# Cross-attention on one core: another order of all operations, and a PSUM bank of its own for the fourth energy product

## The chip, the core and the metric

The kernel runs on one core of one Trainium2 chip. The core has a matrix engine (TensorE; PE in the profile, with its weight loads as PEld), three engines for elementwise work (VectorE, DVE; ScalarE, ACT; GpSimd, POOL), a queue that issues transfers (SyncE, SP), an on-chip memory SBUF and an accumulator memory PSUM of eight banks, each 128 partitions by 512 float32 values. Matmuls write PSUM; ACT and DVE read and write it; POOL works on SBUF alone.

The metric is the device time of one execution in microseconds. The kernel before takes 1973.53 us (median of 3 runs, 1973.33 to 1973.71).

## The reference

For each of 32 samples, with `x` and `y` (the context) of 256 channels by 1024 positions:

```python
x_q = einsum('oc,bcn->bno', w_qk, y)
x_k = einsum('oc,bcn->bon', w_qk, x)
x_v = einsum('oc,bcn->bon', w_v, x) + b_v[None, :, None]
energy = einsum('bnc,bcm->bnm', x_q, x_k)
attention = softmax(energy, axis=-1)
attention = attention / (1e-07 + attention.sum(axis=1, keepdims=True))
x_r = einsum('bcn,bnm->bcm', x_v, attention)
x_r = relu(einsum('oc,bcn->bon', w_t, x - x_r) + b_t[None, :, None])
return x + x_r
```

## The kernel before

**Numbers.** Each float32 operand of a matmul is split into a rounded part (HIGH) and the remainder (LOW). `product` makes one block product of three matmuls, high by high, high by low and low by high, into one bank. So each name with a P below, and each A, is three matmuls of 128x128 weights by 512 columns.

**Blocks of seven products.** The keys (`k`, from `w_qk` twice and x), the energies (`E0` to `E3`) and the part of the output that comes from x (`x`) are made as 2 by 2 blocks with seven products P1 to P7 in place of eight. `chain` says in which bank each accumulates: P1, then P6, then P7 and last P4 in bank `a`, P2 in `b`, P5 and then P3 in `c`. Between them ACT copies the running sum of bank `a` to SBUF three times: `r1` after P1, `r2` after P6, `r3` after P7. DVE then adds these copies to the other banks: `c11` = b + r1, `c22` = c + r3 (before P3 comes on top of c), `c12` = c + r2 (after P3). The fourth block, 21, is what stands in bank `a` after P4.

**One sample's work.** An energy `E<p>` gives a pair of tiles of 128 rows by 1024 columns: tile 2p lies in banks 0 and 1, tile 2p+1 in banks 2 and 3. For these the smallest value of each row is needed, and DVE takes it in the instruction that makes a block: `c22`, `c11`, `c12` add and take the minimum at once; for block 21, which needs no addition, `m21` (`energy_least`) reads bank `a` with a row of zeros as second operand. Then, for tile n with halves h of 512 columns (one bank each): `exp<n>` on ACT over both banks, with the row sums; `ri<n>` on DVE, their reciprocals; for each half `h<n><h>` on ACT (HIGH of the attention weights), `l<n><h>` on DVE (LOW; it needs the result of `h`) and `sum<n><h>` on DVE (adds the tile to the column sums `acc`). `A<n><c><h>` multiplies the values `uf` with these weights into banks 4 to 7. The next pair's P1 can start when the bank that it writes has been read by `h`, `l` and `sum`.

**The rest.** `V<q><half>` makes the values (12 matmuls of 256 columns each), `vh` (ACT) and `vl` (DVE) split them. `cols`, `inv` and `turn` (DVE) turn the column sums into reciprocals, `div<c>` (DVE) divides, `join<c>` (POOL) adds the x part, `pos<c>` (ACT) is the relu, `add<c>` is a transfer on POOL's queue that adds x, `st<c>` (SP) stores. The next sample's operands are prepared meanwhile: `xh`, `yh`, `xTh`, `ysh`, `khD`, `kTh` on ACT, `xl`, `yl`, `xTl`, `ysl`, `klD`, `kTl0`, `kTl1` and the sums `xT`, `ys`, `kT2` on POOL.

**What sets the order.** Three lists of names, `FIRST`, `STEADY` (repeated for samples 1 to 29) and `LAST`. A `+` before a name means the next sample, a `-` the one before. `InOrder` keeps each engine to the order of the list; between engines each instruction waits for what it depends on, and any two accesses of ACT, DVE and PE to one PSUM bank keep the list's order too, two reads included.

Of the kernel before, what the change touches and what calls it, by code (L numbers as in the profile page):

```python
# [17 lines left out]
def kernel(  # L18
# [739 lines left out]
    for c in range(KC):  # L758
# [13 lines left out]
        ys01 Sgram Swt ys03 ys02 Scorner Swtc ys04 Sgh0 Stp Sgh1 Sbvw Fxh0 Sgl xh1 Sgraw  # L772
        Fyh Ssq Fxl0 yh00 Svh Gh12 FHH0 yh01 Fyl yl00 FHL0 FHH1 FLH0 Svl Fxl1 FLH1 yl01
        FHL1 ysh0 Fraw11 Fkh12 V01 V00 V11 Fkh11 ysl0 V10 kT1 Sth Fraw22 vh0 kT2 Th12
        Fkh22 Fkl12 Fkl11 ldy1 kT3 Fkl22 kh21 kT4 kl21 FE11 FE00 yh11 yh10 kTh0 vh1 FE10
        FE01 vl0 vl1 Fmin1 Stl Gl12 kTh1 Sbias Tl12 ys11 exp1 kTl0 Fmin0 +ldx0 ri1 Gs1
        +xT1 h10 sum11 Gs2 kTl1 l10 sum10 FX11 FX01 FX00 E1P1 exp0 ri0 h11 h01 FX10 h00
        E1r1 Fxw0 E1P6 Gh22 l11 l01 sum00 Ts1 ys13 l00 ys12 E1P2 sum01 E1r2 Fxw1 E1P7 E1r3
        E1P5 E1P4 A110 Gs3 E1c11 Ts2 ys14 ysh1 Gl22 E1c22 E1m21 +xh0 exp3 Ts4 E1P3 Ts3
        yl11 Gs4 E1c12 yl10 A101 A010 A111 A100 ri3 h30 exp2 ysl1 h31 sum30 l30 E2P1 A000  # L780
        E2r1 sum31 ri2 E2P6 +ldx1 A011 h21 Th22 l31 sum20 l21 sum21 E2r2 E2P7 h20 GhS E2P5
        l20 E2r3 E2P4 E2c22 E2m21 +xh1 E2P2 ThS E2P3 +xl0 E2c11 +xT3 E2c12 +xTh0 exp5 ri5
        +ldy0 h50 A300 A001 exp4 h51 A301 A200 sum50 l50 E3P1 ri4 E3r1 sum40 +xT2 sum51
        GlS h41 sum41 l51 A500 E3P6 E3r2 A310 h40 +yh00 E3P7 l41 E3r3 +xl1 +ys03 +xT4
        +ys01 E3P5 +yh01 +xTh1 l40 +ldy1 E3c22 E3P4 E3P2 E3m21 TlS +xTl0 E3c11 +ys02 exp7
        E3P3 A311 +ys13 +xTl1 Tl22 E3c12 ri7 h70 sum70 A400 A201 A210 A211 h71 exp6 l70
        l71 +kP1 A510 ri6 sum71 +yl00 +ys04 +kr1 +ysh0 +ys11 +ys12 sum61 +kP6 A511 A501
        h61 +kr2 +yl01 +ys14 l61 +kP7 h60 +yh11 +kP5 sum60 +kr3 l60 +kc22 +ysl0 +kP2 +kc11
        +kP3 +kc12 A401 A410 +kP4 +khD +yl11 +kT1 +yh10 +kh21 A701 A411 +kT2 +klD A700
# [3 lines left out]
        E0P1 -cols ysh1 kTh1 -inv --st0 kTl1 -A610 -A601 -A711 E0r1 kTh0 -turn E0P6 -div0
        E0r2 E0P2 --st1 +ldx0 -A611 kTl0 E0P7 -div1 E0r3 E0P5 E0c22 E0P4 yl10 E0m21 E0c11
        V11 exp1 ri1 E0P3 h10 -join0 ysl1 V10 V00 h11 E0c12 exp0 sum10 l10 sum11 ri0 vh1
        sum01 E1P1 E1r1 h00 V01 h01 vl1 E1P6 E1r2 xP1 E1P7 vh0 +ldx1 l00 l01 sum00 l11
        E1r3 xr1 +xh0 E1P5 E1P2 E1P4 vl0 E1c22 A111 E1m21 exp3 xP2 xP6 E1c11 E1P3 -join1
# [6 lines left out]
        E3c22 A210 E3P4 A510 -add0 +ys11 +xTl1 E3m21 +ysh0 +yh11 E3P3 exp7 E3c12 ri7 A511
        A200 A301 A410 sum70 h70 exp6 l70 sum71 ri6 +kP1 +kr1 A201 sum61 sum60 h61 +yh01
        +kP6 +kr2 h71 h60 A710 l61 +kP5 +kP7 +yh10 +kr3 l60 +kc22 A501 +yl11 +yl00 +ys12
        +ysl0 +ys13 +yl01 +ys14 +kP2 +kP3 l71 A500 +kc11 +khD +kc12 A401 +kP4 A400 A411
        A700 +kT1 +kh21 +kT3 +kT2 +klD +kl21 +kT4 A701 A600
    """
# [80 lines left out]
```

## Time and profile before

| | |
|---|---|
| median of 3 runs | 1973.53 us |
| the profiled execution | 1973.25 us |
| its span, first to last instruction | 1971.5 us |
| PE busy | 1893.3 us (96%) |
| DVE busy | 1606.0 us (81%) |
| ACT busy | 1430.9 us (73%) |
| POOL busy | 1395.1 us (71%) |
| mean granted TensorE clock | 0.999 |

The profile counts an instruction from its start to its end. Matmuls overlap: the next one starts before the one before has ended, and so the distance between starts is what a matmul costs. All instructions of the three compute engines and of PE bear line 62, since `InOrder` issues them; they are told apart by operation and tile: `banks<-gf,yd` is a P1, P2 or P4 of an energy, `banks<-gf,ysum` one of its P3, P5, P6, P7, `banks<-efs,uf` an A, `banks<-xf,gws` a key product, `banks<-xf,tws` an x product, `banks<-vws,xf` a V. On DVE `efs` is an `l`, `acc` a `sum`, and `CUSTOM_DVE_ANT_0` a `c` or `m21` of an energy. On ACT `efs` is an `h`, `banks<-banks,small` an `exp`, `rs<-banks` an `r`.

### The profile page before, as it was taken

The numbers are of one execution on the slowest core, as the hardware profiler recorded it, in microseconds if no ns is written. First come the engines' busy times: TensorE is split into PE (matmuls) and PEld (weight loads), VectorE is DVE, ScalarE is ACT, GpSimd is POOL, SyncE is SP. The second block draws the span as 40 slices with busy tenths as digits, with TensorE's granted clock in tenths as the row PEclk, the third lists the DMA queues.
The fourth block names the chain that finished last, engine by engine and source line by source line (L and its number), as shares of the span: only waits on it lengthen the run. The fifth ranks groups of instructions, "written<-read, shape, count | busy, mean of one in ns | idle before, by whom it ended". The sixth has DMA issues, their size and how long they took to land. (4 is left out here: it accounts for less than half of the span.)

```text
span 1971.5 us, 25233 instructions
## 1 busy us (share of the span) xinstructions
PE 1893.3 (96%) x8680; PEld 1495.7 (76%) x8680; DVE 1606.0 (81%) x3044; ACT 1430.9 (73%) x2223; POOL 1395.1 (71%) x975
## 2 busy tenths in 40 slices
PE   9999999999999999999999999999999999999998
PEld 7777777777777777777777777777777777777776
DVE  6878888788887788887888878888788887888877
ACT  7777777777777777767777777777777777777665
POOL 8876777767677676777677776777767777676672
PEclk9999999999999999999999999999999999999999
DMA  2122212222122231222221232212222122221222
GB/s 94 36 82 75 75 44 75 75 75 75 47 71 75 75 82 47 65 76 83 78 52 56 75 86 75 66 53 76 75 75 75 44 75 75 75 75 50 59 75 75
DMA packets 46722, 136.78 MB, mean 69 GB/s; under 512 B 4480, under 2 KB 5376, under 8 KB 46592
## 3 DMA queue, kind: packets, MB, share of 16 engines
q1 hardware_dynamic: 37248, 102.25, 15.0%
q0 software_dynamic: 8928, 32.51, 9.8%
q8 instruction: 68, 1.11, 0.2%
q14 instruction: 62, 0.51, 0.1%
q10 hardware_dynamic: 416, 0.39, 0.1%
HBM read 101.58 MB, written 33.55 MB: 69 GB/s over the span
## 5 line engine op out<-in xcount | busy, mean ns | idle before, releaser
L62 PE MATMUL banks<-efs,uf 128*128 128x512 f32 x3072 | 780.5, 390 | 0.0
L62 PEld LDWEIGHTS banks<-efs,uf 128*128 128x128 f32 x3072 | 576.7, 188 | 124.2
L62 DVE SCALAR_TENSOR_TENSOR efs<-banks,small,efs 128x512 fp32r<-128x512 f32 x512 | 376.1, 746 | 131.6 <-ACT efs L62 131.5
L62 PE MATMUL banks<-gf,ysum 128*128 128x512 f32 x1524 | 421.1, 398 | 26.8 <-ACT rs L62 25.8
L62 ACT ACTIVATE efs<-banks,small 128x512 fp32r<-128x512 f32 x512 | 340.3, 693 | 122.5 <-DVE acc L62 68.2
L62 ACT COPY rs<-banks 128x512 f32<-128x512 f32 (+1 forms) x475 | 278.0, 585 | 188.2 <-PE banks L62 175.6
L62 PEld LDWEIGHTS banks<-gf,ysum 128*128 128x128 f32 x1524 | 274.1, 188 | 113.3 <-ACT rs L62 55.1
L62 ACT ACTIVATE banks<-banks,small 128x1024 f32<-128x1024 f32 x256 | 278.1, 1086 | 110.0 <-DVE small L62 109.8
L62 PE MATMUL banks<-gf,yd 128*128 128x512 f32 x1158 | 333.8, 400 | 23.3 <-DVE efs L62 20.0
L62 DVE SCALAR_TENSOR_TENSOR acc<-banks,small,acc 128x512 f32<-128x512 f32 x448 | 328.5, 745 | 15.2 <-ACT efs L62 6.9
L62 POOL TENSOR_TENSOR xf<-raws,xf 128x1024 fp32r<-128x1024 f32 x62 | 149.7, 2415 | 208.8 <-ACT xf L62 208.8
L62 PEld LDWEIGHTS banks<-gf,yd 128*128 128x128 f32 x1158 | 206.0, 188 | 99.2 <-DVE efs L62 32.4
L62 POOL TENSOR_TENSOR sums<-raws 128x256 f32<-128x256 f32 (+1 forms) x188 | 187.0, 1003 | 80.5 <-DMA raws<-in_ctx_dram 76.4
L62 POOL TENSOR_TENSOR gf<-sums,gf 128x1024 fp32r<-128x1024 f32 x95 | 227.3, 2408 | 2.1
L62 PE MATMUL banks<-xf,gws 128*128 128x512 f32 x651 | 195.3, 417 | 19.8 <-DVE efs L62 19.7
L62 PEld LDWEIGHTS banks<-vws,xf 128*128 128x128 f32 x1536 | 196.3, 190 | 8.2
L62 PE MATMUL banks<-vws,xf 128*128 128x256 f32 x1536 | 198.5, 282 | 0.0
L62 DVE CUSTOM_DVE_ANT_0 banks<-banks,rs 128x512 f32<-128x512 f32 x254 | 179.0, 705 | 22.2 <-PE banks L62 16.9
L62 PEld LDWEIGHTS banks<-xf,gws 128*128 128x128 f32 x651 | 110.4, 188 | 92.8 <-DVE efs L62 51.8
L62 PE MATMUL banks<-xf,tws 128*128 128x512 f32 x651 | 168.3, 389 | 0.0
L62 POOL TENSOR_TENSOR ysum<-sums,ysum 128x1024 fp32r<-128x1024 f32 x64 | 158.7, 2480 | 8.2 <-ACT ysum L62 8.2
L62 ACT CAST gf<-sums 128x1024 fp32r<-128x1024 f32 x95 | 99.9, 1053 | 76.1 <-DVE sums L62 76.0
(105 smaller groups left out, 2338.6 us busy)
## 6 DMA issues: line engine op xcount, KB each, us to landing
raws<-in_x_dram SPq DMA_DIRECT2D x66, 512.0 KB, 3.2
raws<-in_ctx_dram SPq DMA_DIRECT2D x63, 512.0 KB, 3.8
z<-in_x_dram POOLq DMA_DIRECT2D x62, 512.0 KB, 5.4
out_dram<-z SPq DMA_DIRECT2D x62, 512.0 KB, 4.0
out_dram<-z SPq DMA_DIRECT2D x4, 256.0 KB, 2.0
xe<-in_ctx_dram SPq DMA_DIRECT2D x1, 512.0 KB, 6.7
z<-in_L_xattn_w_t_dram ACTq DMA_DIRECT2D x1, 256.0 KB, 4.4
z<-in_L_xattn_w_v_dram SPq DMA_DIRECT2D x1, 256.0 KB, 5.1
```

The lines of the kernel that those rows point to most:

```text
L62: self.last = getattr(self.engine, name)(*args, **kwargs)
```

## The change

All energies get other banks: `a` is bank 3 and `d` bank 2 (before: `a` bank 2, `d` bank 3). P4 no longer accumulates on bank `a`: it starts a sum of its own in `d`. `c22` now writes to bank `a` instead of `d`. `m21` with its row of zeros goes, and `c21` comes in its place: it adds `r3` to bank `d` and takes the minimum in the same instruction. The tiles lie where they lay.

```diff
-    zeros_row = nc.const_aps.tensor(0.0, [P, MB], F32)
...
-        where = {1: "a", 2: "b", 5: "c", 6: "a", 7: "a", 4: "a", 3: "c"}
+        where = {1: "a", 2: "b", 5: "c", 6: "a", 7: "a", 4: "d" if "d" in bank else "a", 3: "c"}
         for i, w in where.items():
             words[f"{name}P{i}"] = lambda b, i=i, w=w: product(
-                banks[:, bank[w]], left(i), right(i), i in (1, 2, 5)
+                banks[:, bank[w]], left(i), right(i), i in (1, 2, 5) or w == "d"
             )
...
-    EB = dict(a=2, b=0, c=1, d=3)
+    EB = dict(a=3, b=0, c=1, d=2)
...
-    def energy_least(b, p):
-        dve.tensor_tensor_reduce(
-            out=eb["a"],
-            in0=eb["a"],
-            in1=zeros_row,
...
-        return banks[:, EB["a"] : EB["a"] + 2] if n % 2 else banks[:, EB["b"] : EB["b"] + 2]
+        at = EB["bd"[n % 2]]
+        return banks[:, at : at + 2]
...
-        word(f"E{p}c22", energy_block, p, 3, "c", "d", "mB", None)
+        word(f"E{p}c22", energy_block, p, 3, "c", "a", "mB", None)
         word(f"E{p}c12", energy_block, p, 2, "c", "c", "m0", "mA")
-        word(f"E{p}m21", energy_least, p)
+        word(f"E{p}c21", energy_block, p, 3, "d", "d", "m1", "mB")
...
     STEADY = """
...
-        E2P3 -pos1 A110 E2c12 exp5 A311 ri5 A010 A001 sum50 h50 exp4 A300 l50 +yh00 E3P1
...
+        E2P4 xc12 l20 E2r3 E2c22 xw21 +xh1 E2c21 A101 E2P2 A110 E2P3 exp5 E2c11 ri5 E2c12
+        h51 exp4 +ldy0 h50 l51 A001 sum51 A010 ri4 +xTl1 A311 A310 +ys01 h41 E3P1 A300
```

The number of instructions of each kind on each engine is the same before and after. The three lists are new from end to end; in the steady list `sum` stands ahead of `h` for 9 of the 16 halves before, and for 4 of 16 in the change. Three places show how the work moves.

First, PE from the third pair's energy to the fourth's. Before, the `ysum` row just ahead of the long `efs` row is P3, the `yd` row ahead of it P4, and the `yd` row behind the long one the fourth pair's P1:

```order
L62 MATMUL banks<-gf,ysum 128x512 x6
L62 MATMUL banks<-efs,uf 128x512 x3
L62 MATMUL banks<-gf,yd 128x512 x3
L62 MATMUL banks<-gf,ysum 128x512 x3
L62 MATMUL banks<-efs,uf 128x512 x15
L62 MATMUL banks<-gf,yd 128x512 x3
L62 MATMUL banks<-efs,uf 128x512 x6
L62 MATMUL banks<-gf,ysum 128x512 x3
```

In the change the first `yd` row here is P4, the second P2, and the third the next pair's P1:

```order
L62 MATMUL banks<-gf,ysum 128x512 x6
L62 MATMUL banks<-gf,yd 128x512 x3
L62 MATMUL banks<-efs,uf 128x512 x3
L62 MATMUL banks<-gf,yd 128x512 x3
L62 MATMUL banks<-efs,uf 128x512 x3
L62 MATMUL banks<-gf,ysum 128x512 x3
L62 MATMUL banks<-efs,uf 128x512 x12
L62 MATMUL banks<-gf,yd 128x512 x3
L62 MATMUL banks<-efs,uf 128x512 x3
L62 MATMUL banks<-gf,ysum 128x512 x9
```

P4 has moved ahead of P2 and P3, and 27 matmuls in place of 21 lie from the start of P4 to the next P1. Behind P1 one A in place of two lies ahead of P6 (`ysum`).

Second, DVE at the same place, from the reciprocal of tile 5 (the first `RECIPROCAL`) on. Before:

```order
L62 RECIPROCAL small<-small 128x1
L62 SCALAR_TENSOR_TENSOR acc<-banks,small,acc 128x512
L62 SCALAR_TENSOR_TENSOR efs<-banks,small,efs 128x512
L62 RECIPROCAL small<-small 128x1
L62 SCALAR_TENSOR_TENSOR acc<-banks,small,acc 128x512
L62 SCALAR_TENSOR_TENSOR efs<-banks,small,efs 128x512
```

In the change:

```order
L62 RECIPROCAL small<-small 128x1
L62 ISA banks,small<-banks,rs,small 128x512
L62 ISA small 128x1
L62 SCALAR_TENSOR_TENSOR efs<-banks,small,efs 128x512
L62 SCALAR_TENSOR_TENSOR acc<-banks,small,acc 128x512
L62 RECIPROCAL small<-small 128x1
L62 SCALAR_TENSOR_TENSOR efs<-banks,small,efs 128x512
```

`c12` (the `ISA` pair: the addition, and the reading of its minimum) now stands behind the reciprocal, and `l` ahead of `sum`.

Third, POOL, from the `add` transfers to the first energy of the next sample. Before:

```order
L62 DMA z<-in_x_dram 128x1024 x2
L62 TENSOR_TENSOR sums<-raws 128x256
L62 TENSOR_TENSOR xf<-sums,xf 128x1024
L62 TENSOR_TENSOR yd<-raws,yd 128x2x2x128
L62 TENSOR_TENSOR yd<-raws,yd 128x256
L62 TENSOR_TENSOR sums<-sums,raws 128x256
L62 TENSOR_TENSOR ysum<-sums,ysum 128x1024
L62 TENSOR_TENSOR sums<-raws 128x256
L62 TENSOR_TENSOR yd<-raws,yd 128x2x2x128
L62 TENSOR_TENSOR sums<-raws,sums 128x256
L62 TENSOR_TENSOR sums<-sums 128x512
L62 TENSOR_TENSOR gf<-sums,gf 128x1024 x3
```

In the change (behind the last row come the same three `gf` rows, `klD`, `kTl1` and `kTl0`):

```order
L62 DMA z<-in_x_dram 128x1024
L62 TENSOR_TENSOR xf<-sums,xf 128x1024
L62 TENSOR_TENSOR sums<-sums,raws 128x256
L62 TENSOR_TENSOR sums<-raws,sums 128x256
L62 TENSOR_TENSOR sums<-sums,raws 128x256
L62 TENSOR_TENSOR yd<-raws,yd 128x2x2x128
L62 TENSOR_TENSOR sums<-raws 128x256
L62 TENSOR_TENSOR sums<-raws,sums 128x256
L62 DMA z<-in_x_dram 128x1024
L62 TENSOR_TENSOR yd<-raws,yd 128x256
L62 TENSOR_TENSOR ysum<-sums,ysum 128x1024
L62 TENSOR_TENSOR sums<-sums 128x512
```

The two `add` transfers no longer stand together: one has moved down past the `xf` and six more instructions. The last three rows ahead of the `gf` rows are now `yl00`, `ysl0` and `kT2`.

More of the change, by code (lines that the diff above doesn't have):

```diff
@@ L771 @@
     FIRST = """
[L772 to L789, printed above, removed]
@@ L791 @@
+        +yh10 A610 +klD +kTl1 +kh21
     """
     STEADY = """
[L793 to L797, printed above, removed]
@@ L804 @@
[L804 to L808, printed above, removed]
+        E0P1 E0r1 yh11 ysh1 -A700 -A701 -A611 E0P6 -div1 kTl0 -A601 kl21 -A600 E0r2 E0P7
@@ L809 @@
+        sum60 +kr2 +kP7 +kr3 A710 +ysh0 +kP2 +kc22 h71 +kc11 +kP3 +kc12 -st1 A610 +kP4
+        -add0 +yl00 +kT1 +ysl0 +kT2 +kT3 l71 +khD ++ldx0 -st0 +kT4 +kTh0 +klD +kTh1 cols
+        A511 A400 +kh21 inv turn +kTl1 A501 A411 A401 A711
     """
     LAST = """
[L811 to L813 removed]
@@ new lines @@
+        xl1 -A311 -A101 -l20 -sum20 -E2r3 -E2c22 -E2P2 -E2c21 xTh0 xTh1 -exp5 -E2c11 -ri5
+        -A110 -E2P3 xl0 -A001 -A000 -A010 -A301 -h51 -h50 ldy1 -E2c12 ldy0 xTl0 -l51
+        -sum51 -exp4 -E3P1 -ri4 -h41 -E3r1 -A300 -E3P6 -l50 -sum41 -h40 -l41 -E3r2 yh01
+        -sum50 -l40 -sum40 -E3P5 --pos0 -E3P7 -A200 -E3r3 -E3c22 -E3P2 xTl1 ys01 ys11 ys02
+        --add0 --pos1 -E3P4 -A310 -A201 -E3P3 -E3c21 -A501 -A211 yh11 -exp7 -E3c11 -A500
+        -A210 -ri7 -E3c12 -h70 -l70 -sum70 kP1 yh10 -exp6 -ri6 -sum71 ys12 ys14 ys13 yl10
```

99 lines of the change are left out of this document (54 added, 45 removed).

## The prediction, written before the result was known

> **What bounds the kernel now.** I read the page first (engines' shares), then PE in order of time over one sample, then the groups, and then DVE and ACT in order of time at PE's two longest stops.
>
> ```profile
> PE 1893.3 (96%) x8680; PEld 1495.7 (76%) x8680; DVE 1606.0 (81%) x3044; ACT 1430.9 (73%) x2223; POOL 1395.1 (71%) x975
> ```
>
> PE looks full, but its ends overlap. PE in order of time (start, length, how many) over one sample, which runs from its first energy product at 623.55 to the next sample's at 684.46, 60.91 us:
>
> ```profile
> 620.15 3.56 PE L62 MATMUL banks<-efs,uf 128*128 128x512 f32 x15
> 623.55 0.91 PE L62 MATMUL banks<-gf,yd 128*128 128x512 f32 x3
> ...
> 628.40 1.60 PE L62 MATMUL banks<-gf,ysum 128*128 128x512 f32 x6
> 630.03 0.96 PE L62 MATMUL banks<-gf,yd 128*128 128x512 f32 x3
> ...
> 632.96 3.03 PE L62 MATMUL banks<-vws,xf 128*128 128x256 f32 x24
> 635.83 0.86 PE L62 MATMUL banks<-gf,yd 128*128 128x512 f32 x3
> ...
> 653.93 0.84 PE L62 MATMUL banks<-gf,yd 128*128 128x512 f32 x3
> 654.61 0.84 PE L62 MATMUL banks<-gf,ysum 128*128 128x512 f32 x3
> 655.29 3.56 PE L62 MATMUL banks<-efs,uf 128*128 128x512 f32 x15
> 659.50 0.98 PE L62 MATMUL banks<-gf,yd 128*128 128x512 f32 x3 [0.64 <-DVE efs L62]
> 660.32 1.55 PE L62 MATMUL banks<-efs,uf 128*128 128x512 f32 x6
> ...
> 662.39 0.86 PE L62 MATMUL banks<-gf,yd 128*128 128x512 f32 x3
> 664.09 1.65 PE L62 MATMUL banks<-gf,ysum 128*128 128x512 f32 x6 [0.83 <-ACT rs L62]
> ...
> 666.26 0.84 PE L62 MATMUL banks<-gf,yd 128*128 128x512 f32 x3
> ...
> 668.30 2.88 PE L62 MATMUL banks<-efs,uf 128*128 128x512 f32 x12
> 671.81 0.97 PE L62 MATMUL banks<-xf,gws 128*128 128x512 f32 x3 [0.62 <-DVE efs L62]
> ...
> 673.45 0.96 PE L62 MATMUL banks<-xf,gws 128*128 128x512 f32 x3
> ...
> 679.01 0.85 PE L62 MATMUL banks<-efs,uf 128*128 128x512 f32 x3
> ...
> 684.46 0.93 PE L62 MATMUL banks<-gf,yd 128*128 128x512 f32 x3
> ```
>
> Fifteen matmuls take 3.40 us from the first start to the next group's: 0.227 us each, so a product of three costs 0.68. Twenty-four V matmuls take 2.87: 0.12 each. A sample has, by the code, 222 of the first kind (four energies, keys and x part of 21 each, 96 for the output) and 48 of the second: 50.4 + 5.7 = 56.1 us. So PE loses 60.9 - 56.1 = **4.8 us a sample**; nothing in the change alters the 56.1. Where it loses them, from the same rows (distance between starts less 0.227 a matmul):
>
> - A, ahead of the fourth pair's P1 (energy `E3`) at 659.50: 655.29 + 15 x 0.227 = 658.69, so 0.81, and 0.14 more because a product that had to wait takes 0.82 to the next start: 0.95.
> - B, the fourth pair's P7 at 664.09: 1.70 - 0.68 = 1.02, and 0.13 of the same start-up: 1.15.
> - C, the keys' P1 at 671.81: 3.51 - 2.72 = 0.79.
> - D, the keys' other products: 671.81 to 679.01 with 27 matmuls, 7.20 - 6.12 = 1.08.
> - E, the first pair's P4 at 630.03: 1.63 - 1.36 = 0.27, and the start-up: 0.39.
>
> A to E make 4.36; about 0.45 lies in shorter stops (the second pair's P7, mostly). All are waits of PE for ACT and DVE, whose own busy time leaves room (81% and 73%). What they wait for at A, DVE and then ACT in order of time:
>
> ```profile
> 654.82 0.76 DVE L62 CUSTOM_DVE_ANT_0 banks<-banks,const-float32-0.0,small 128x512 f32<-128x512 f32 x1 [0.51 <-PE banks L62]
> 656.91 0.16 DVE L62 RECIPROCAL small<-small 128x1 f32<-128x1 f32 x1 [0.59 <-ACT banks L62]
> 657.11 0.75 DVE L62 SCALAR_TENSOR_TENSOR acc<-banks,small,acc 128x512 f32<-128x512 f32 x1
> 658.69 0.75 DVE L62 SCALAR_TENSOR_TENSOR efs<-banks,small,efs 128x512 fp32r<-128x512 f32 x1 [0.84 <-ACT efs L62]
> ```
> ```profile
> 655.67 1.09 ACT L62 ACTIVATE banks<-banks,small 128x1024 f32<-128x1024 f32 x1 [0.40 <-DVE small L62]
> 657.97 0.69 ACT L62 ACTIVATE efs<-banks,small 128x512 fp32r<-128x512 f32 x1 [1.10 <-PE banks L62]
> 672.81 0.59 ACT L62 COPY rs<-banks 128x512 f32<-128x512 f32 x1 [0.75 <-PE banks L62]
> ```
>
> The third pair's P4 starts at 653.93, `m21` 0.89 later, `exp5` 0.85 after that, `ri5` 1.24, then `sum50`, `h50` (the profile names PE as what it waited for, but `sum50`, on the same bank, ended at 657.86, 0.11 before), `l50`, and P1 0.81 after `l50`'s start: 5.57 us from P4 to the next P1. PE has 21 matmuls, 4.76 us, to cover them. The difference, 0.81, is A. C is the same: from the fourth pair's P4 at 666.26, 21 matmuls cover 4.76 and the keys start 5.55 later. So a loss here is a chain's length less the work that PE finds in the list meanwhile.
>
> **The change part by part.** *Counts and prices.* No instruction goes or comes; `c21` takes the form of `c12`, and `m21` cost as much:
>
> ```profile
> L62 DVE CUSTOM_DVE_ANT_0 banks<-banks,const-float32-0.0,small 128x512 f32<-128x512 f32 x127 | 96.4, 759 | 39.8 <-PE banks L62 30.3
> L62 DVE CUSTOM_DVE_ANT_0 banks<-banks,rs,small 128x512 f32<-128x512 f32 x127 | 96.3, 759 | 26.7 <-PE banks L62 25.9
> L62 ACT ACTIVATE efs<-banks,small 128x512 fp32r<-128x512 f32 x512 | 340.3, 693 | 122.5 <-DVE acc L62 68.2 <-PE banks L62 37.0 <-DVE small L62 15.4
> ```
>
> 759 ns each: nothing. All gain or loss is PE's waiting.
>
> *E, P4 in its own bank.* It no longer waits for `r3`. Its new bank was last read by `kl21` on DVE, which stands between `div1` and `div0` and should end some 1 us ahead of P4. E goes: 0.39 saved (bounds 0 and 0.39).
>
> *A and C, the cover.* In the change the fourth pair's P1 comes 27 matmuls, 6.12 us, after P4's start. The chain: `c21` 0.89 after P4, `exp5` 0.85, `ri5` 1.24, `h51` 0.20, and `l51` 0.72 later, at 3.90. But `c12` stands ahead of `l51` on DVE and needs P3, which starts 2.72 after P4 and is ready at 3.65; `c12` puts `l51` to about 4.35. `sum51` follows 0.67 behind, and P1 0.81 after its start: 5.83. It fits with 0.3 to spare, so A becomes 0 (bounds 0 and 0.4). The keys' P1 again lies 27 matmuls behind its P4; there `c21` waits for `c22`, which waits for `r3` (behind `yh00` and `xTh0` on ACT), and starts about 1.2 after P4; the rest is the same, some 5.8 to 6.0 against 6.12. C becomes 0 (0 to 0.4). This, and not a shorter chain, is where I see the gain: `l` and `sum` still read one bank one after the other.
>
> [...]
>
> *B and D, the steps of bank `a`.* From one product in bank `a` to the next one there a copy on ACT must fit. The keys' P1 at 671.81 is read at 672.81, the copy takes 0.59, and P6 follows at 673.45: 1.64, and about 1.52 where P1 has no start-up of its own. With one other product between, PE has 1.36. So each step with a single product between costs 0.16 to 0.28 and a start-up of 0.13, say 0.35. The new order has six such places a sample: the third pair's P7 (an x product between), the fourth pair's P6 (one A) and P7 (P5), the keys' P6 and P7, and the keys' P3, which needs `c22` after `r3` (about 2.3 us against 2.04). 6 x 0.35 = 2.1. For the second pair's P7 (`r2` behind `vh0` on ACT) I add 0.2, and 0.25 for what stays everywhere: 2.55, where B, D and the short stops have 1.15 + 1.08 + 0.45 = 2.7 now. Bounds of this part: 1.5 (the steps at 0.2) and 3.4 (two late copies more).
>
> *POOL ahead of the next sample.* P1 of the next sample needs `klD`, the first of the three `gf` rows. In the change all of this stands in one line on POOL, from the `add` transfer that waits for `pos1`, which ACT runs right behind the fourth pair's `r3`:
>
> ```profile
> L62 POOL TENSOR_TENSOR gf<-sums,gf 128x1024 fp32r<-128x1024 f32 x95 | 227.3, 2408 | 2.1
> L62 POOL TENSOR_TENSOR ysum<-sums,ysum 128x1024 fp32r<-128x1024 f32 x64 | 158.7, 2480 | 8.2 <-ACT ysum L62 8.2
> L62 POOL TENSOR_TENSOR xf<-sums,xf 128x1024 fp32r<-128x1024 f32 x62 | 153.6, 2477 | 1.5 <-ACT xf L62 1.5
> L62 POOL TENSOR_TENSOR yd<-raws,yd 128x512 fp32r<-128x512 f32 (+1 forms) x126 | 133.3, 1107 | 1.6 <-ACT yd L62 1.6
> L62 POOL DMA_DIRECT2D z<-in_x_dram x62 | 53.8, 878 | 108.0 <-ACT z L62 108.0
> L62 POOL TENSOR_TENSOR sums<-sums,raws 128x256 f32<-128x256 f32 x63 | 50.7, 805 | 2.4
> L62 POOL TENSOR_TENSOR sums<-sums 128x512 f32<-128x512 f32 x32 | 41.4, 1294 | 121.9 <-DVE sums L62 121.9
> ```
>
> Two `add` 1.76, `xf` 2.48, five small `sums` of about 0.85, two `yd` 2.21, `ysum` 2.48, `kT2` 1.29, `klD` 2.41: 16.9 us. Counted from the third pair's P4, the fourth pair's `r3` ends near 11.2 and `pos1` near 12.3, so `klD` ends near 29.1. PE's work from that P4 to the next sample is 27.2, and with 1.7 of stops 28.9: I take 0.2 (bounds 0 and 1.0). Before, POOL stood idle 121.9 us in 31 samples ahead of `kT2`, so there it had 4 us to give.
>
> *Sum.* A 0, C 0, E 0, the steps 2.55, POOL 0.2: 2.75 us a sample against 4.85. That is 2.1 saved, 31 times (the first and the last sample together count as one, having parts of the same stops): 65 us. 1973.25 - 65 = 1908 for an execution like the profiled one, whose time is 0.3 us under the median: **1908 us**. All terms at their lower bounds: 1.5 a sample, 3.35 saved, 1869. At their upper ones: 3.4 + 0.8 + 1.0 = 5.2, 0.35 more than now, 1984.
>
> **The rivals.**
>
> *Only the bank acts, the covers come to nothing.* The spare 0.3 at A and C is small, and one transfer or one late ACT instruction eats it; if A and C move to the next product, E's 0.39 stays: 31 x 0.39 = 12 us, **1961 us**. For it: ACT is strictly in order, and three waits stand ahead of `r2`. Against: 27 matmuls in place of 21 are 1.36 us more cover at both places.
>
> *PE hardly waits.* If ACT's back-to-back starts (672.81 and the like: less than the length of one) keep up better than I reckon, only some 0.3 to 0.8 us a sample stay, 4.2 saved: **1843 us**. Against: with one product between two steps the 1.56 us are a floor.
>
> [...]
>
> *The stops only move.* Same sum in other places, **1973 us**. For it: DVE and ACT have the same work. Against: the two longest stops are worked out as covered.
>
> *Slower: POOL's line becomes the bound.* From the point at which `klD` comes 2.3 us later than I reckon (2.1 saved and 0.2 already counted), each further us costs 31. The second y transfer, asked for only when `xl1` has run, or a later `pos1`, would do it; 1 us beyond is **2004 us**. For it: the line has no slack, where before it had 4 us. Against: POOL's groups have steady durations and its line is counted whole.
>
> **How the numbers follow.** Forecast 0.63, only the bank 0.12, hardly any wait 0.08, moved stops 0.06, slower 0.11. A difference under 0.2% (4 us) can't be told from none. Faster by more: 0.63 + 0.12 + 0.08 = 0.83; within: 0.06; slower: 0.11. The likeliest case's own range is 1885 to 1940; to hold 8 in 10 with the 1961 partly in and half of the fast case: 1875 to 1958.
>
> **What would show it.** In the changed kernel PE's row of P4 follows without a wait for `rs`; the stops ahead of the fourth pair's P1 and of the keys' P1 are under 0.3 us; single-cover steps (`gf,ysum`, `xf,gws`) show 0.2 to 0.35 each; ACT's `efs` waits for DVE's `acc` fall well under 68.2 us; POOL's wait for `DVE sums` ahead of `kT2` falls from 121.9 us toward nothing, and its idle time sits ahead of the `add`. A period of 58.8 us a sample is the forecast. Wrong would be: PE waiting for `POOL gf` for more than 1 us a sample, or a stop of over 0.8 us at A or C.

## The result, and the profile after

The changed kernel takes 1892.92 us (median of 4 runs, 1892.67 to 1893.59), the kernel before 1973.47 us on the same chip (4 runs, 1973.33 to 1973.71). The ratio is 0.9592 with a 95% interval from 0.9576 to 0.9609: 81 us less, where 65 were forecast. The span of the profiled execution fell by as much, from 1971.5 to 1890.5 us.

The first part of the page of the changed kernel:

```profile
PE 1869.4 (99%) x8680; PEld 1499.5 (79%) x8680; DVE 1609.0 (85%) x3044; ACT 1432.2 (76%) x2223; POOL 1400.0 (74%) x975
```

The counts of instructions are the same, and DVE, ACT and POOL are busy for as long as before, within 5 us. What changed is when PE waits. PE of the changed kernel in order of time, over the sample that runs from 599.17 to 657.64 (start, length, how many):

```profile
599.17 0.88 PE L62 MATMUL banks<-gf,yd 128*128 128x512 f32 x3
...
604.00 1.55 PE L62 MATMUL banks<-gf,ysum 128*128 128x512 f32 x6
605.39 1.53 PE L62 MATMUL banks<-gf,yd 128*128 128x512 f32 x6
...
626.22 0.84 PE L62 MATMUL banks<-xf,tws 128*128 128x512 f32 x3
627.36 1.65 PE L62 MATMUL banks<-gf,ysum 128*128 128x512 f32 x6 [0.30 <-ACT rs L62]
628.85 0.86 PE L62 MATMUL banks<-gf,yd 128*128 128x512 f32 x3
...
632.27 2.88 PE L62 MATMUL banks<-efs,uf 128*128 128x512 f32 x12
634.99 0.84 PE L62 MATMUL banks<-gf,yd 128*128 128x512 f32 x3
635.67 0.84 PE L62 MATMUL banks<-efs,uf 128*128 128x512 f32 x3
636.51 2.62 PE L62 MATMUL banks<-gf,ysum 128*128 128x512 f32 x9
638.97 0.85 PE L62 MATMUL banks<-efs,uf 128*128 128x512 f32 x3
639.66 1.52 PE L62 MATMUL banks<-gf,yd 128*128 128x512 f32 x6
...
645.78 0.84 PE L62 MATMUL banks<-xf,gws 128*128 128x512 f32 x3
646.46 0.84 PE L62 MATMUL banks<-efs,uf 128*128 128x512 f32 x3
647.30 2.61 PE L62 MATMUL banks<-xf,gws 128*128 128x512 f32 x9
649.75 0.85 PE L62 MATMUL banks<-efs,uf 128*128 128x512 f32 x3
650.44 1.91 PE L62 MATMUL banks<-xf,gws 128*128 128x512 f32 x6
652.19 0.85 PE L62 MATMUL banks<-efs,uf 128*128 128x512 f32 x3
...
657.64 0.62 PE L62 MATMUL banks<-gf,yd 128*128 128x512 f32 x2
```

The sample takes 58.47 us; it was 60.91. Stop A is gone: the fourth pair's P1 at 634.99 comes 2.72 us after the twelve A matmuls started at 632.27, which is 12 x 0.227. Stop C is gone in the same way (645.78, behind the last of the `efs` rows). Stop E is gone: P4 and P2 at 605.39 follow 1.39 after P7 and P5, of which 1.36 is work. B was 1.15; now the nine matmuls P6, P5, P7 from 636.51 take 2.46 for 2.04 of work, and P6 itself comes 0.16 late. The largest stop that is left stands ahead of the third pair's P7 at 627.36, 0.46 late and with 0.13 of start-up: 0.59.

Such stops are compared below for all kernels as means over samples 4 to 27 of each trace, from the distances between starts, less 0.227 us for a matmul of 512 columns and 0.12 for one of 256. The start-up of the product that waited is in them:

| us a sample | before | changed |
|---|---|---|
| period | 60.98 | 58.48 |
| all stops of PE | 4.83 | 2.33 |
| first pair's P4 | 0.33 | 0.01 |
| second pair's P7 | 0.26 | 0.02 |
| third pair's P7 | 0 | 0.60 |
| fourth pair's P1 | 0.91 | 0.01 |
| fourth pair's P6, P7 | 0, 1.14 | 0.28, 0.26 |
| keys' P1 | 0.90 | 0 |
| keys' other products | 0.92 | 0.94 |

The 2.50 us a sample make 72.5 us over the 29 periods from the second sample to the last but one. The other 8.4 of the 80.9 us between the two spans lie at the two ends: 2.5 before the second sample begins, 2.6 in the last period, and 3.4 behind the first product of the last sample.

The groups of waits of the changed kernel (engine, what it wrote, what it waited for: us in total, times, longest), and the group of `h` on the page:

```profile
PE banks L62 <- ACT rs L62: 9.2, 29, 0.6
PEld banks L62 <- POOL gf L62: 5.1, 28, 0.5
ACT efs L62 <- DVE small L62: 22.3, 89, 0.4
POOL sums L62 <- DVE sums L62: 1.2, 2, 0.9
...
L62 ACT ACTIVATE efs<-banks,small 128x512 fp32r<-128x512 f32 x512 | 339.4, 689 | 34.8 <-DVE small L62 22.3
```

ACT's `h` no longer waits for DVE's `acc` (68.2 us before): with `sum` behind `h` in the list, DVE waits for ACT instead (`acc` for `efs` 20.2 us, 6.9 before). POOL's 121.9 us of waiting ahead of `kT2` are 1.2, so POOL's line now runs through to the end of the sample, as POOL in order of time shows (first `add`, then `kT2`, then `klD`, `kTl1`, `kTl0`):

```profile
641.11 0.88 POOL L62 DMA_DIRECT2D z<-in_x_dram  x1 [2.84 <-ACT z L62]
...
654.04 1.30 POOL L62 TENSOR_TENSOR sums<-sums 128x512 f32<-128x512 f32 x1
655.29 7.13 POOL L62 TENSOR_TENSOR gf<-sums,gf 128x1024 fp32r<-128x1024 f32 x3
```

`klD`, the first of the last three, takes 2.41 us and so ends at 657.70. PE starts the next sample at 657.64, with a matmul that doesn't need `klD`. From the `add` to that end it is 16.6 us; the prediction had counted 16.9.

### The profile page after: what moved, and what is told of

Same layout as the page of the kernel before. It is cut to its first block, busy times and chain, and to the rows that moved or that the text cites. A ratio compares the mean times of both kernels' runs of the same rounds, so it can differ in the third digit from the quotient of the medians.

```text
span 1890.5 us, 25202 instructions
## 1 busy us (share of the span) xinstructions
PE 1869.4 (99%) x8680; PEld 1499.5 (79%) x8680; DVE 1609.0 (85%) x3044; ACT 1432.2 (76%) x2223; POOL 1400.0 (74%) x975
## 5 line engine op out<-in xcount | busy, mean ns | idle before, releaser
L62 DVE SCALAR_TENSOR_TENSOR acc<-banks,small,acc 128x512 f32<-128x512 f32 x448 | 329.8, 742 | 21.7 <-ACT efs L62 20.2
L62 PE MATMUL banks<-gf,yd 128*128 128x512 f32 x1158 | 319.1, 392 | 0.4 <-DVE efs L62 0.2
L62 POOL TENSOR_TENSOR xf<-sums,xf 128x1024 fp32r<-128x1024 f32 x62 | 157.6, 2543 | 189.4 <-PE banks L62 116.7
L62 POOL TENSOR_TENSOR sums<-raws 128x256 f32<-128x256 f32 (+1 forms) x188 | 173.6, 931 | 112.3 <-DMA raws<-in_ctx_dram 112.3
L62 PEld LDWEIGHTS banks<-gf,yd 128*128 128x128 f32 x1158 | 212.4, 188 | 49.9 <-POOL gf L62 5.1
L62 DVE CUSTOM_DVE_ANT_0 banks<-banks,rs,small 128x512 f32<-128x512 f32 x254 | 192.7, 759 | 27.9 <-PE banks L62 11.0
L62 PE MATMUL banks<-vws,xf 128*128 128x256 f32 x1536 | 194.3, 283 | 0.0
L62 PE MATMUL banks<-xf,gws 128*128 128x512 f32 x651 | 189.5, 412 | 3.0 <-DVE small L62 0.2
L62 PE MATMUL banks<-xf,tws 128*128 128x512 f32 x651 | 183.0, 390 | 0.0
L62 POOL TENSOR_TENSOR ysum<-sums,ysum 128x1024 fp32r<-128x1024 f32 x64 | 154.4, 2412 | 22.2 <-ACT ysum L62 22.2
```

What stands on the lines that cost most here:

```text
L62: self.last = getattr(self.engine, name)(*args, **kwargs)
```

## The experiments

Several theories stood against each other from the start. By the first, the gain is **cover**: the chain from P4 over ACT and DVE to the next P1 is as long as ever, and the new order puts more products beside it. By the others it is the **bank** alone, or the **order of the readers** of a half (`h`, `l`, `sum`), or slack on POOL. Each kernel was timed in three rounds against the kernel before on its own chip (1973.5 to 1974.3 us).

### The bank alone, in the order before

The lists of before, with the banks and `c21` of the change. P4 starts a sum in `d`, so the halves of odd tiles change places in the banks, and the names of their halves are exchanged with them.

```diff
-        where = {1: "a", 2: "b", 5: "c", 6: "a", 7: "a", 4: "a", 3: "c"}
+        where = {1: "a", 2: "b", 5: "c", 6: "a", 7: "a", 4: "d" if "d" in bank else "a", 3: "c"}
...
-        word(f"E{p}m21", energy_least, p)
+        word(f"E{p}c21", energy_block, p, 3, "d", "d", "m1", "mB")
```

> The order before, with the change's bank: P4 in a bank of its own, c21 in place of m21. The bank of P1 is then that of the odd tiles' other half, so in these tiles the two halves change places in the lists. Theory 1 (a stop of PE is the length of a chain less the work that the list has for PE meanwhile; the new cover is the order's): only the wait of the first pair's P4 for r3 goes, 0.4 us a sample, 12 us: 1957 to 1965. Theory 2 (the bank is the gain): P4 of all pairs is free of r3, and most of the 80 us come: 1900 to 1930. A theory that only both together gain anything gives 1973.

Measured: 1984.99 us (1984.71 to 1985.63), ratio 1.0056 (1.0041 to 1.0071): slower, not faster. The stop ahead of the first pair's P4, 0.33, did go, but 0.19 us appeared ahead of the second pair's P1: the chain to that P1 runs from `r3` over `c22`, `c21` and `exp1`, and it doesn't begin with P4. `c21` starts 4.67 us after the first pair's P6, and before, `m21` started 4.69 after it. For more than half of the 0.33, PE only came earlier to the same wait. The rest of the loss is no property of the bank, as a run further down shows: the keys' P1 waits 1.21 us in place of 0.90, since the exchanged half of tile 7 writes its weights where a product still reads, and the second sample begins 6.1 us later (81.06 us after the start of the span, 74.94 before).

### The new order without the bank

The changed kernel, with P4 on bank `a` again and so behind `r3` in the lists, and `m21` back. By this the two halves of an odd tile change places in the banks.

```diff
-        where = {1: "a", 2: "b", 5: "c", 6: "a", 7: "a", 4: "d" if "d" in bank else "a", 3: "c"}
+        where = {1: "a", 2: "b", 5: "c", 6: "a", 7: "a", 4: "a", 3: "c"}
...
-        sum01 E1r1 h00 vl1 h01 vh0 +ldx1 l01 sum00 E1P6 vl0 l00 E1r2 E1P4 xP1 E1P7 +xh0
-        E1r3 E1P5 E1c22 xP2 E1P2 E1c21 xr1 -pos0 E1P3 xP6 A111 xP5 exp3 E1c11 xr2 +xT2
+        sum01 E1r1 h00 vl1 h01 vh0 +ldx1 l01 sum00 E1P6 vl0 l00 E1r2 xP1 E1P7 +xh0 E1r3
+        E1P5 E1P4 E1c22 xP2 E1P2 E1c21 xr1 -pos0 E1P3 xP6 A111 xP5 exp3 E1c11 xr2 +xT2
```

> The new order, with P4 accumulating on bank a behind r3 as before, and m21; where the new order has P4 ahead of r3 (second and third pair) P4 moves right behind it or behind P5. Theory 1: P4 then waits for r3 in all four pairs, from the changed kernel's trace 0.33 + 1.1 + 0.28 + 0.37 = 2.1 us a sample, so most of the gain goes: 1945 to 1965. Theory 2 (bank alone): all of it goes, 1973 or more. Theory 3 (ACT and DVE reading different banks is the gain, which this kernel keeps): 1895 to 1915.

Measured: 1953.43 us (1952.94 to 1955.70), ratio 0.9898 (0.9883 to 0.9913). A and C stay at 0; the stops are 4.18 a sample. The bank, with the places that it allows P4, is worth 60 us in this order: 1.85 in each sample, 54 in all, and the rest at the two ends. PE in order of time shows where (second pair's P7 and P5, then P4):

```profile
638.05 0.85 PE L62 MATMUL banks<-xf,tws 128*128 128x512 f32 x3
639.32 1.65 PE L62 MATMUL banks<-gf,ysum 128*128 128x512 f32 x6 [0.41 <-ACT rs L62]
640.96 0.96 PE L62 MATMUL banks<-gf,yd 128*128 128x512 f32 x3
```

P4 here stands 1.64 behind P7 for 1.36 of work, and P7 is late by 0.59, because P4 no longer stands between P6 and P7. In the changed kernel it does, and is the second product that covers `r2`. So the bank gains by setting P4 free as filling: without it, in the mean, 0.32, 0.27, 0.27 and 0.36 us are lost ahead of the four P4 of a sample, and 0.69 ahead of the second pair's P7.

### Two products less beside stop A

```diff
-        h51 exp4 +ldy0 h50 l51 A001 sum51 A010 ri4 +xTl1 A311 A310 +ys01 h41 E3P1 A300
+        h51 exp4 +ldy0 h50 l51 A001 sum51 A010 ri4 +xTl1 +ys01 h41 E3P1 A311 A310 A300
```

> The changed kernel with the two products A311 and A310 moved, in the steady list, from ahead of the fourth pair's P1 to behind it: 21 matmuls in place of 27 between the third pair's P4 and that P1, as before the change. Theory 1: the chain (5.75 us from P4 in the changed kernel's trace) is then longer than its cover of 4.76: a stop of 1.0 to 1.1 us comes back ahead of that P1, 0.28 ahead of P6 goes, net 0.8 a sample, 29 times: 1910 to 1922. Theories 2 and 3: bank and reads are untouched, 1893 within 4 us.

Measured: 1920.19 us (1920.06 to 1920.38), ratio 0.9727 (0.9713 to 0.9742). PE in order of time, from the third pair's P4 to the fourth pair's P1:

```profile
638.87 0.84 PE L62 MATMUL banks<-gf,yd 128*128 128x512 f32 x3
...
642.27 1.52 PE L62 MATMUL banks<-efs,uf 128*128 128x512 f32 x6
644.71 0.93 PE L62 MATMUL banks<-gf,yd 128*128 128x512 f32 x3 [0.92 <-DVE acc L62]
```

P1 comes 1.08 us later than the six A matmuls at 642.27 need: the 1.36 taken away, less 0.28 that had been spare. With its start-up the stop is 1.18 in the mean, while the 0.28 ahead of P6 went with the two products that now stand there. This is the cover theory in both directions. From P4 to P1 it is 5.84 us.

### One product more between two steps

```diff
-        h21 h30 E2r1 sum20 A000 xP4 +xTh1 l21 E2P6 xc22 E2r2 h20 sum21 xP3 l30 E2P7 E2P5
+        h21 h30 E2r1 sum20 A000 xP4 +xTh1 l21 E2P6 xc22 E2r2 h20 sum21 xP3 l30 E2P5 E2P7
```

> The changed kernel with the third pair's P5 ahead of its P7 in the steady list, so that two products lie between P6 and P7 in place of one. Theory 1: the stop of 0.60 us ahead of that P7 goes, and nothing later uses it up: 29 x 0.5 to 0.6 = 15 to 17 us, 1876 to 1879. Rival (POOL's line to the next sample's first product is as long as the sample, so that PE waits for it instead): 1889 to 1893.

Measured: 1885.58 us (1885.42 to 1886.45), ratio 0.9552 (0.9536 to 0.9568): faster than the changed kernel by 7.3 us, between the two theories. The stop ahead of the third pair's P7, 0.60, is gone; 0.33 appears ahead of the fourth pair's P1. The chain to that P1 starts at `r3`, and `r3` came no earlier than before: 2.96 us after the pair's P6, in the changed kernel 2.85. So half of the gain at this step was given back at the end of its chain.

### `sum` ahead of `h` again

```diff
-        h51 exp4 +ldy0 h50 l51 A001 sum51 A010 ri4 +xTl1 A311 A310 +ys01 h41 E3P1 A300
-        E3r1 l41 sum41 E3P6 +xl1 h40 E3P5 E3r2 E3P7 +yh00 +xTh0 sum50 l50 sum40 l40 +ldy1
+        sum51 h51 exp4 +ldy0 sum50 h50 l51 A001 A010 ri4 +xTl1 A311 A310 +ys01 sum41 h41
+        E3P1 A300 E3r1 l41 E3P6 +xl1 h40 E3P5 E3r2 E3P7 +yh00 +xTh0 l50 sum40 l40 +ldy1
...
```

> The changed kernel with one difference in the steady list: for six halves (tile 4 half 1, both halves of 5 and 6, tile 7 half 0) the sum stands just ahead of h again, as in the list before; products, banks and every other place are as changed. Theory 1 (the place of h, l and sum counts, since ACT runs in order and its next copy r stands queued behind an h that waits for a sum): l comes 0.5 to 0.7 us later at the fourth pair's P1 and at the keys' P1, where nothing or 0.3 us is spare, and the copies behind h40 and h60 come later too: 1.5 to 2.5 us a sample, 29 samples, 1936 to 1965 us. Theory 2 (only the number of products that cover a chain counts, the order of the three readers of a half is nearly free): at most 0.5 us a sample, 1893 to 1908 us.

Measured: 1972.66 us (1972.39 to 1973.30), ratio 0.9996 (0.9986 to 1.0005). Six names, and the whole gain is gone: more than the first theory had expected. ACT at the fourth pair in order of time, then PE (P1 and P6):

```profile
658.84 0.69 ACT L62 ACTIVATE efs<-banks,small 128x512 fp32r<-128x512 f32 x1 [1.89 <-DVE acc L62]
...
661.72 0.69 ACT L62 ACTIVATE efs<-banks,small 128x512 fp32r<-128x512 f32 x1 [0.52 <-DVE acc L62]
662.30 0.58 ACT L62 COPY rs<-banks 128x512 f32<-128x512 f32 x1
```
```profile
660.36 0.97 PE L62 MATMUL banks<-gf,yd 128*128 128x512 f32 x3 [0.38 <-DVE efs L62]
661.17 0.86 PE L62 MATMUL banks<-efs,uf 128*128 128x512 f32 x3
662.93 2.61 PE L62 MATMUL banks<-gf,ysum 128*128 128x512 f32 x9 [0.91 <-ACT rs L62]
```

`h51` waits 1.89 us for `sum51`, the chain from the third pair's P4 (653.68) to P1 grows from 5.84 to 6.68, and stop A is back with 0.67. The second effect is larger: `h41` waits for `sum41`, the copy `r1` stands behind it on ACT and starts at 662.30, though P1 was ready about 0.9 after its start at 660.36, and P6 comes 1.19 late. At the keys the same thing costs 1.51. ACT works through its list in order, and so the 0.52 us for which `h41` waited went on to the copy queued behind it.

### The place of `sum` alone, in the order before

```diff
-        E2P3 -pos1 A110 E2c12 exp5 A311 ri5 A010 A001 sum50 h50 exp4 A300 l50 +yh00 E3P1
+        E2P3 -pos1 A110 E2c12 exp5 A311 ri5 A010 A001 h50 exp4 A300 l50 sum50 +yh00 E3P1
...
-        +ldy1 A310 E3P6 sum41 h51 h41 E3P2 E3r2 -pos0 E3P7 l41 E3r3 E3P5 +xTh1 E3c11 l51
+        +ldy1 A310 E3P6 h51 h41 E3P2 E3r2 -pos0 E3P7 l41 sum41 E3r3 E3P5 +xTh1 E3c11 l51
...
-        A200 A301 A410 sum70 h70 exp6 l70 sum71 ri6 +kP1 +kr1 A201 sum61 sum60 h61 +yh01
+        A200 A301 A410 h70 exp6 l70 sum70 sum71 ri6 +kP1 +kr1 A201 sum61 sum60 h61 +yh01
```

> The kernel before with one difference in its steady list: for three halves (both at which its longest stops began, 50 and 70, and 41, whose h stood behind its sum ahead of the copy r2) the sum stands right behind l instead of ahead of h. Banks, products and all other places are those of before. Theory 1 (the place of the sum alone is worth a good part of the gain, because ACT and its queued copies no longer wait): 0.2 us less at the fourth pair's P1, 0.8 less at its P7, 0.2 less at the keys' P1, 1.2 us a sample in 29, 1930 to 1955 us. Theory 2 (in the order before the chains move on to the next product, as with its bank alone; only the new order as a whole brings it): 1962 to 1980 us.

Measured: 1942.66 us (1942.58 to 1946.94), ratio 0.9844 (0.9830 to 0.9859): three names gain 31 us. Stop B is 0.27 where it was 1.14. ACT of the kernel before at `h41` and `r2`:

```profile
662.87 0.69 ACT L62 ACTIVATE efs<-banks,small 128x512 fp32r<-128x512 f32 x1 [1.07 <-DVE acc L62]
663.46 0.58 ACT L62 COPY rs<-banks 128x512 f32<-128x512 f32 x1
```

and of this kernel at the same two, with `h51` ahead of `h41` in the first row:

```profile
651.81 1.27 ACT L62 ACTIVATE efs<-banks,small 128x512 fp32r<-128x512 f32 x2
653.39 0.59 ACT L62 COPY rs<-banks 128x512 f32<-128x512 f32 x1 [0.31 <-PE banks L62]
```

Before, `r2` waited for `h41`, which waited 1.07 us for `sum41`; now it waits for nothing but its product. A and C fall by only 0.09 and 0.13: there P1 now waits for `sum`, which comes hardly earlier than `l` did. In the runs here these two stops went only with more cover.

### Bank and place of `sum` together, in the order before

The edit is that of the first experiment and the last one in one kernel.

> The order before with the bank for P4 (1985 us, of which some 15 us come from the exchange of halves that this order needs) and with the same three sums behind l. Theory 1 (bank and place of the sum act on different chains and add up): as much less as the place of the sum brings without the bank, 1940 to 1965 us. Theory 2 (each lets the other act, as the bank did in the new order): more than that, below 1935 us. Theory 3 (neither matters in the order before): 1975 to 1990 us.

Measured: 1978.05 us (1976.78 to 1979.64), ratio 1.0019 (1.0009 to 1.0029): the third theory's figure, but for a reason of its own. ACT's row for the first half of tile 7:

```profile
674.69 0.69 ACT L62 ACTIVATE efs<-banks,small 128x512 fp32r<-128x512 f32 x1 [1.34 <-PE banks L62]
```

It waits for a product that still reads the place where it writes its weights, and the keys' P1 is 1.88 late. So that product, A301, was moved two places up (the diff is against the kernel just measured):

```diff
-        E3c22 A210 E3P4 A510 -add0 +ys11 +xTl1 E3c21 +ysh0 +yh11 E3P3 exp7 E3c12 ri7 A511
-        A200 A301 A410 h70 exp6 l70 sum70 sum71 ri6 +kP1 +kr1 A201 sum61 sum60 h61 +yh01
+        E3c22 A210 E3P4 A510 -add0 +ys11 +xTl1 E3c21 +ysh0 +yh11 E3P3 exp7 E3c12 ri7 A301
+        A511 A200 A410 h70 exp6 l70 sum70 sum71 ri6 +kP1 +kr1 A201 sum61 sum60 h61 +yh01
```

> The order before with the bank for P4 and the three sums behind l (1978 us), and A301 three products earlier in the steady list: with the exchanged halves, h of tile 7 writes the weights that A301 reads, and had to wait for it. Theory 1 (that wait is the 1.1 us at the keys' P1 by which it stands above the same order on the old bank, and the bank itself is worth 0.1 us a sample here): 1.1 us a sample less, 1943 to 1950 us, no faster than the 1942.7 us on the old bank, since about 6 us of first sample and head stay. Theory 2 (the bank gains its 0.3 us a sample once the exchange costs nothing): 1930 to 1938 us.

Measured: 1945.93 us (1945.76 to 1947.19), ratio 0.9856 (0.9841 to 0.9871), within the first theory's 1943 to 1950. The stop at the keys' P1 fell by 1.05, the period is 59.87 with the bank and 59.87 without it, the sum of the stops 3.72 in both. In the order before, with these three `sum` moved, the bank by itself is worth nothing: the 0.33 us saved ahead of the first pair's P4 come back as 0.17 ahead of the second pair's P1 and in smaller parts further on.

### POOL's line made longer

```diff
+        word(f"ysl{q}twice", y_sums_low, q)
...
-        -add0 +yl00 +kT1 +ysl0 +kT2 +kT3 l71 +khD ++ldx0 -st0 +kT4 +kTh0 +klD +kTh1 cols
+        -add0 +yl00 +kT1 +ysl0 +ysl0twice +kT2 +kT3 l71 +khD ++ldx0 -st0 +kT4 +kTh0 +klD
```

> The changed kernel with ysl0 issued twice in succession on POOL in the steady list (the same values are computed again): 2.41 us more in POOL's line between the add transfer and klD, and nothing else. Theory 1 (in the changed kernel that line has no slack: klD ends as PE comes to the next sample's P1, so a further us on POOL costs a us of each sample): 2.1 to 2.4 us a sample, 29 samples, 1953 to 1963 us, with PE waiting for POOL's gf ahead of the next sample's first product. Theory 2 (POOL still has slack there, since PE hardly waits for it): 1893 to 1905 us.

Measured: 1979.44 us (1977.25 to 1983.65), ratio 1.0030 (1.0020 to 1.0040). The line has no slack: PE waits ahead of the second matmul of the next sample's P1, 2.49 us a sample. But 86.5 us more for 2.41 us on POOL in each of 29 samples is 17 too many. At least a part of them lies behind the wait. PE in order of time in one sample (first matmul of P1, the other two, the nine A matmuls, P6), and then in the next:

```profile
502.35 0.39 PE L62 MATMUL banks<-gf,yd 128*128 128x512 f32 x1
504.94 1.10 PE L62 MATMUL banks<-gf,yd 128*128 128x512 f32 x2 [2.20 <-POOL gf L62]
505.84 3.48 PE L62 MATMUL banks<-efs,uf 128*128 128x512 f32 x9
509.16 0.85 PE L62 MATMUL banks<-gf,ysum 128*128 128x512 f32 x3
...
567.40 0.73 PE L62 MATMUL banks<-gf,yd 128*128 128x512 f32 x2 [2.11 <-POOL gf L62]
567.98 2.21 PE L62 MATMUL banks<-efs,uf 128*128 128x512 f32 x9
```

The same nine matmuls take 3.48 us in the one and 2.21 in the other. The section on the hardware takes this up.

### Three more moves, and where they lead

The kernel with one product more between two steps, and the same done at other places (A300, A200, and on ACT `ysh0`):

```diff
-        h51 exp4 +ldy0 h50 l51 A001 sum51 A010 ri4 +xTl1 A311 A310 +ys01 h41 E3P1 A300
-        E3r1 l41 sum41 E3P6 +xl1 h40 E3P5 E3r2 E3P7 +yh00 +xTh0 sum50 l50 sum40 l40 +ldy1
-        E3r3 A200 E3P4 E3P2 A210 -pos1 A301 E3c22 E3c21 exp7 E3c11 ri7 h70 E3P3 A510 +yh01
+        h51 exp4 +ldy0 h50 l51 A001 sum51 A010 ri4 +xTl1 A311 A310 +ys01 h41 A300 E3P1
+        E3r1 l41 sum41 A200 E3P6 +xl1 h40 E3P5 E3r2 E3P7 +yh00 +xTh0 sum50 l50 sum40 l40
+        +ldy1 E3r3 E3P4 E3P2 A210 -pos1 A301 E3c22 E3c21 exp7 E3c11 ri7 h70 E3P3 A510
...
```

> The kernel with the third pair's P5 ahead of its P7 (1885.6 us), and three more moves in the steady list: A300 from behind the fourth pair's P1 to ahead of it, A200 from behind its P7 to ahead of its P6, and ysh0 on ACT from behind the keys' r3 to ahead of it. Theory 1 (a stop is a chain's length less the work in between, so the 0.33 us stop that appeared ahead of the fourth pair's P1 goes, and the keys' P1 keeps enough cover): 0.25 to 0.4 us a sample less, 1874 to 1880 us. Theory 2 (POOL's line, with klD at its end, is by now the bound of the sample, and PE only waits elsewhere): no gain, 1883 to 1888 us, with a stop at the next sample's first product.

Measured: 1883.89 us (1883.52 to 1885.29), ratio 0.9543 (0.9527 to 0.9559). That beats both kernels, but the step itself brought 1.7 us of the 6 to 12 expected, too little to tell from none. The stop ahead of the fourth pair's P1 went from 0.33 to 0, and 0.27 appeared ahead of the keys' P1, which had lost one product of cover. The time is the second theory's, but its reason isn't seen: no stop over 0.1 stands at the next sample's first product.

Then, in that kernel, `c12` was put ahead of `ri7`, to shorten the chain to the keys' P1:

```diff
-        +ldy1 E3r3 E3P4 E3P2 A210 -pos1 A301 E3c22 E3c21 exp7 E3c11 ri7 h70 E3P3 A510
-        +yh01 A500 A211 E3c12 +ys11 +ys03 -add1 +xTl0 +ys02 +ys04 +ys12 exp6 +yh10 A201
+        +ldy1 E3r3 E3P4 E3P2 A210 -pos1 E3c22 E3P3 A301 E3c21 exp7 E3c11 E3c12 ri7 h70
+        A510 +yh01 A500 A211 +ys11 +ys03 -add1 +xTl0 +ys02 +ys04 +ys12 exp6 +yh10 A201
```

> The 1883.9 us kernel, and in the steady list the fourth pair's P3 ahead of A301 and its c12 ahead of ri7 (so that DVE has done c12 before h70 comes). Theory 1 (its 0.27 us stop at the keys' P1 is the chain over c12, sum70 and l70 on DVE, which becomes 0.6 us shorter): the stop goes, 0.25 to 0.35 us a sample, 1874 to 1877 us. Theory 2 (ri7 comes later by as much as c12 comes earlier, or the later parts of the sample take the gain back): 1881 to 1886 us.

Measured: 1889.43 us (1889.10 to 1890.22), ratio 0.9569 (0.9555 to 0.9583): slower by 5.5 us than without the move; the first theory expected 7 to 10 us less. DVE of this kernel from `c12` to `sum70`:

```profile
641.99 0.76 DVE L62 CUSTOM_DVE_ANT_0 banks<-banks,rs,small 128x512 f32<-128x512 f32 x1
642.66 0.14 DVE L62 DVE_READ_ACCUMULATOR2_ANT small<- 128x1 f32 x1
642.66 0.16 DVE L62 RECIPROCAL small<-small 128x1 f32<-128x1 f32 x1
643.59 0.75 DVE L62 SCALAR_TENSOR_TENSOR acc<-banks,small,acc 128x512 f32<-128x512 f32 x1 [0.77 <-ACT efs L62]
```

`sum70` waits 0.77 us for `h70` on ACT. `c12` had run for free beside `h70`; ahead of `ri7` it delays `ri7`, `h70` and all behind by 0.20 us a sample, and the stop ahead of the keys' P1 grows from 0.27 to 0.48. The second theory had `ri7` coming later, but the time lies above its 1881 to 1886 too. The program lets the two readers of this bank have it only one after the other, and the trace shows the price of that here, the 0.77 us for which `sum70` waits until `h70` has read the bank; no run shows what would happen if it didn't wait.

Last, in the kernel with `c12` early, a product was moved from ahead of the keys' P1 to behind it:

```diff
-        A510 +yh01 A500 A211 +ys11 +ys03 -add1 +xTl0 +ys02 +ys04 +ys12 exp6 +yh10 A201
-        sum70 l70 ri6 h61 +kP1 A410 sum71 +yl01 +ys13 +ys14 +kr1 h60 sum61 l61 +kP6 +kP5
+        A510 +yh01 A500 A211 +ys11 +ys03 -add1 +xTl0 +ys02 +ys04 +ys12 exp6 +yh10 sum70
+        l70 ri6 h61 +kP1 A201 A410 sum71 +yl01 +ys13 +ys14 +kr1 h60 sum61 l61 +kP6 +kP5
```

> The kernel with c12 early, and A201 from ahead of the keys' P1 to behind it, so that two products lie between the keys' P1 and P6. Theory 1 (the chain to the keys' P1 now has about 0.4 us to spare and A201 takes 0.68 of it, while the stop at P6 with its start-up, 0.4 us, goes): 0.1 to 0.2 us a sample less than with c12 early alone, 3 to 6 us. Theory 2 (kP3, on which POOL's klD and so the next sample hang, comes no earlier by it): within 2 us of it.

Measured: 1913.42 us (1913.23 to 1913.57), ratio 0.9690 (0.9674 to 0.9706). This kernel no longer computes the same: A201 now stands behind `h61`, which writes tile 6's weights into the place of tile 2's, so it multiplies with a part of the wrong weights and has a stop of 0.40 us of its own. Only the stop ahead of the keys' P1 can be read: 1.15 us, against 0.48 with `c12` early. The 0.68 us of one product taken away came back whole as waiting, since there was nothing to spare.

## Why the prediction came out as it did

**What bounds the kernel.** The 56.15 us of PE's work a sample did not move (60.98 - 4.83 and 58.48 - 2.33). The whole gain is waiting, as argued.

**A and C** were put at 0 each, with 0.3 us to spare; they are 0.01 and 0. The chain from P4 to P1 was forecast at 5.83 us; the run with less cover, in which P1 has to wait for it, shows 5.84, and so 0.28 to spare. The sums were right, though one step in them was not: `c21` starts 1.23 us after P4 in the mean and not 0.89, since it stands behind `c22` on DVE, which waits for `r3`. That cost nothing only because `c12`, which waits for P3, holds `l51` back just as long, as the prediction had it. And the sentence that cover, and not a shorter chain, makes the gain was half the truth. With fewer products beside it the stop is 1.18; with the old places of `sum` the chain is 6.68 and the cover doesn't suffice. The working had counted `l` right behind `h` without saying that this was a part of the gain.

**B and D** were priced as six places of 0.35, 2.1 in all; the six measure 0.60, 0.28, 0.26, 0.28, 0.28 and 0.38, 2.08 (of the 0.28 at the keys' P7, 0.18 stand ahead of the P5 in between). That the sum fits so well is partly luck, for the steps range from 0.26 to 0.60. The largest has a cause that was not priced. At the third pair, P6 starts at 625.52, and ACT has a cast for the next sample, `xTh1`, ahead of the copy `r2`; the cast itself waits for a product that still reads the place it writes:

```profile
625.78 1.05 ACT L62 CAST xf<-sums 128x1024 fp32r<-128x1024 f32 x1 [0.45 <-PE banks L62]
626.74 0.57 ACT L62 COPY rs<-banks 128x512 f32<-128x512 f32 x1
```

What the prediction did not name is why B was so long before: `r2` stood behind an `h` that stood behind a `sum`, and with three `sum` moved, that one among them, B is 0.27 in the old order in place of 1.14.

**E** was to be 0.39, saved by the bank. It is gone in the changed kernel, but the bank alone doesn't save it: without the new order more than half of the wait goes to the next P1, and the rest to later stops. So the rival of the bank alone was mis-sized too: 1961 was its price, 1984.99 was measured, and where the exchanged halves cost nothing, nothing was gained (59.87 and 59.87 a sample, with three `sum` moved). In the new order the bank is worth 1.85 us a sample: in these two orders the free bank helped only where the order uses the freed product as filling.

**POOL** was put at 0.2 and is 0.02; the line is 16.6 us in place of 16.9 and ends as PE arrives. That it has no slack is shown by the run that made it longer. The slower rival's mechanism is real, and its price of 31 us for each us was too low: 36 were paid (86.5 / 2.41), and some 7 of them go, by the author's estimate, to the lower granted clock of that run (0.990 in the mean, 0.999 in the changed kernel).

**The size.** 80.9 us went from the span where 65 were forecast. In the 29 periods 72.5 came in place of 60.9, which is 0.40 a sample more. Two terms were mis-sized there: the second pair's P7, put at 0.2 and measured at 0.02, and POOL's 0.2, measured at 0.02; together 0.36 x 29 = 10. At the P7, `r2` is indeed late behind `vh0`, but with P4 set free two products cover it in place of one. The other 4 us are the two ends, which were counted like two steady samples (4.2 us) and gave 8.4.

**The rivals** that PE hardly waits, and that the stops only move, are both excluded by the 2.33 us that stay of 4.83, nearly all at the six steps.

## What to carry to other kernels

Where an engine runs in order, look at what is queued behind an instruction that waits: a reader that can wait (`sum`) put ahead of one that cannot (`h`) cost 80 us here, though both orders have the same work. Price a stop as the chain's length less the work beside it, and look whether part of a gain reappears at the end of the next chain, as it did in several runs above. In these runs a bank of its own for a product paid only where the order then used that product to fill another wait: it was worth 0 in one order and 1.85 us a sample in the other.
